# Order of the ffn's first products by parts of x, and epsilon as a bias of the layernorm's root

## Chip, core, metric

One core of one Trainium2 chip runs the whole program. The engines are TensorE (PE in the profile; PEld are its weight loads), VectorE (DVE), ScalarE (ACT), GpSimd (POOL) and SyncE (SP, which only issues transfers here). The metric is device time in microseconds for one execution; several executions are made, and the median counts. The outputs must agree with the reference.

## What is computed

x has 2048 rows of 256 numbers, float32. It is normalized row by row, and attention (16 heads of 128) and a small gated ffn with three-valued weights both read the normalized x; both are added to x.

```python
def _layernorm(x, axis=-1, eps=1e-05):
    m = jnp.mean(x, axis=axis, keepdims=True)
    v = jnp.var(x, axis=axis, keepdims=True)
    return (x - m) / jnp.sqrt(v + eps)
...
def _quantize(w):
    gamma = jnp.mean(jnp.abs(w))
    return jnp.clip(jnp.round(w / (gamma + EPS)), -1.0, 1.0)

def _bitlinear(x, w):
    return jnp.matmul(x, _quantize(w).T)
x1 = _bitlinear(x, w1)
x2 = _bitlinear(x, w2)
hidden = jax.nn.sigmoid(x1) * x2
return _bitlinear(hidden, w3)
...
xn = _layernorm(x, axis=-1)
x = x + _L0_attn_ref(xn, L0_attn_Wqkv, L0_attn_Wout) + _L0_ffn_ref(xn, L0_ffn_w1, L0_ffn_w2, L0_ffn_w3)
```

w1 and w2 are 704 x 256, w3 is 256 x 704.

## The kernel before

Rows of x go in four blocks (c = 0 to 3) of 512 (QB), each of four tiles (t) of 128 rows. Everything runs inside a manual schedule: each engine executes its instructions in the order in which the Python code writes them, and waits where it needs another engine's result.

**The start.** `loads` issues the transfers of x and the weights. GpSimd fills a few constants, among them `ident`, the identity matrix for transposes (filled by a memset and a select, masks.py lines 197 and 199) and `ones`. TensorE runs 20 transposes of `ident` into a tile `idle` (L539), whose result nobody reads. `normalized` (L381 and on) makes xn of a block or of half a block: the statistics of each row tile (`bn_stats` L388, `bn_aggr` L389) give mean and variance in `mv`; `ve` is variance plus epsilon (L392, VectorE); `sd` is its root (L394, ScalarE); `r0` is the reciprocal (L396), and one Newton step (L398 to L401), which reads ve again, gives `rstd`; L405 writes xn. It is called five times: for tiles 0 and 1 of block 0, for its tiles 2 and 3, and once for each of the blocks 1, 2 and 3. `turned` transposes xn on TensorE (pxn, L416), and ScalarE copies the result into xnT (L420). Pieces of the first heads' v, q and k are written between these calls (L229, L116, L106), with copies on ScalarE (L235, L121, L110). Meanwhile VectorE quantizes w1, w2 and w3 to w0q, w1q and w2q (`quantize`, L446 to L462), the means of their absolute values coming from ScalarE (L431) and a small product (pg, L438).

**The ffn.** Products of the ffn are made with two parts of each float32 operand: the cast to a shorter type (the high part, xh, L477, ScalarE) and what is left (the low part, xl, L478, VectorE). `halved_x(0)` makes them for block 0, before w3 is quantized and after k piece 0. The ffn has 24 chunks (c, f): four blocks by six slices f of the hidden dimension, 128 wide, where the last slice holds the 64 left of both weights. For each, `hidden` makes ph: for the two weights (j = 0, 1, into the two banks of one PSUM tile) four products each, over the two halves d of the 256 inputs and the two parts i of x (i = 0 high, i = 1 low). In before the order is j outermost, then i = 1 before i = 0, then d, so that the low parts come first (L495). A sigmoid on ScalarE (L501) and a product on VectorE (L502) follow, and the result is halved again (hidh, hidl). `summed` multiplies it with w2q into two banks, pf e = 0 and e = 1 (L518), and runs two chunks behind `hidden`: after the chunks 0 and 1 come k pieces 2 and 3, after chunk 2 comes `summed` of chunk 0. The two banks of pf are those that k pieces 2 and 3 used before; ScalarE's copies of these (kT, L110) set them free. The sg and hid tiles lie in a pool that is opened when the pool of the raw weights is closed, so their first writer waits until the quantization has read the raw weights.

**The attention** follows with 64 blocks of queries (16 heads by 4 blocks): scores (L612), maximum (L617), exponential (L627), an exchange of quarter tiles through DMA (L646), transposition (L680), the product with v (L690), and next heads' products between them. ScalarE's table of functions is loaded three times in all: for the first root, the first sigmoid, and for the exponential before the attention.

The sqrt in L394 takes ve with the default bias, a constant in the instruction.

Of the kernel before, what the change touches and what calls it, by code (L numbers as in the profile page):

```python
# [8 lines left out]
F32 = mybir.dt.float32  # L9
F32R = mybir.dt.float32r  # L10
AF = mybir.ActivationFunctionType
# [3 lines left out]
LN_EPS = 1e-05  # L15
# [4 lines left out]
def layernorm_attention_bitffn_kernel(  # L20
# [14 lines left out]
    nc = tc.nc  # L35
    P = 128
# [5 lines left out]
    KC = DM // P  # L42
# [89 lines left out]
    ws, ts = {}, {}  # L132
# [195 lines left out]
    fw = front.enter_context(tc.tile_pool(name="ffw", bufs=1))  # L328
# [13 lines left out]
    def loads(fraw):  # L342


        def load_x(c: int, lo: int, hi: int, queue):
            queue.dma_start(
                ys[c][:, lo:hi],
                x[c * QB + lo * P : c * QB + hi * P, :].rearrange("(t p) d -> p t d", p=P),
            )

        load_x(0, 0, 1, nc.sync)
        load_x(0, 1, 2, nc.scalar)
        load_weights(0, "v")
        load_x(0, 2, TB, nc.scalar)
        load_x(1, 0, 2, nc.sync)
        load_x(1, 2, TB, nc.scalar)
        load_weights(0, "q")
        load_x(2, 0, TB, nc.sync)
        load_x(3, 0, TB, nc.sync)
        raw = []  # L360
        for i, src in enumerate((w1T, w2T)):
            w = fraw.tile([P, KC, FF], F32, tag=f"w{i}", name=f"w{i}s")
            nc.sync.dma_start(w, src.rearrange("(c p) f -> p c f", p=P))
            raw.append(w)
        w = fraw.tile([P, FC, DM], F32, tag="w2", name="w2s")
        whole = FF // P
        rest = FF - whole * P
        if rest:
            nc.gpsimd.memset(w[:LAST, whole, :], 0.0)
        nc.sync.dma_start(  # L370
            w[:, :whole, :], w3T[: whole * P, :].rearrange("(c p) e -> p c e", p=P)
        )
        if rest:
            nc.sync.dma_start(w[LAST:, whole, :], w3T[whole * P :, :])
        raw.append(w)
        load_weights(0, "k")
        return raw

    xns = {}

    def normalized(fraw, c: int, t0: int = 0, t1: int = TB):  # L381

        y = ys[c]
        m = t1 - t0
        mv = fraw.tile([P, m, 2], F32, tag=f"mv{m}", name=f"mv{c}_{t0}", bufs=2)
        for t in range(t0, t1):
            st = fraw.tile([P, 6], F32, tag="st", name=f"st{c}_{t}", bufs=4)
            nc.vector.bn_stats(st, y[:, t, :])  # L388
            nc.vector.bn_aggr(mv[:, t - t0, :], st)  # L389

        ve = fraw.tile([P, m], F32, tag=f"ve{m}", name=f"ve{c}_{t0}", bufs=2)
        nc.vector.tensor_scalar(ve, mv[:, :, 1], LN_EPS, None, ALU.add)  # L392
        sd = fraw.tile([P, m], F32, tag=f"sd{m}", name=f"sd{c}_{t0}", bufs=2)
        nc.scalar.activation(sd, ve, AF.Sqrt)  # L394
        r0 = fraw.tile([P, m], F32, tag=f"r0{m}", name=f"r0{c}_{t0}", bufs=2)
        nc.vector.reciprocal(r0, sd)  # L396
        e0 = fraw.tile([P, m], F32, tag=f"e0{m}", name=f"e0{c}_{t0}", bufs=2)
        nc.vector.scalar_tensor_tensor(e0, ve, -0.5, r0, ALU.mult, ALU.mult)  # L398
        nc.vector.tensor_tensor(e0, e0, r0, ALU.mult)
        rstd = fraw.tile([P, m], F32, tag=f"rstd{m}", name=f"rstd{c}_{t0}", bufs=2)  # L400
        nc.vector.scalar_tensor_tensor(rstd, e0, 1.5, r0, ALU.add, ALU.mult)  # L401
        if t0 == 0:
            xns[c] = fraw.tile([P, TB, DM], F32, tag="xn", name=f"xn{c}")
        for t in range(t0, t1):
            nc.vector.tensor_scalar(  # L405
                xns[c][:, t, :], y[:, t, :], mv[:, t - t0, 0:1], rstd[:, t - t0 : t - t0 + 1],
                ALU.subtract, ALU.mult,
            )

    def turned(c: int, t0: int = 0, t1: int = TB):  # L410


        pt = ps_s.tile([P, KC, QB], F32, tag="s", name=f"pxn{c}_{t0}")
        for d in range(KC):
            for t in range(t0, t1):
                nc.tensor.transpose(  # L416
                    pt[:, d, bass.ts(t - t0, P)], xns[c][:, t, bass.ts(d, P)], ident
                )
        m = (t1 - t0) * P
        nc.scalar.copy(xnT[:, :, c * QB + t0 * P : c * QB + t0 * P + m], pt[:, :, :m])  # L420
# [5 lines left out]
    def magnitude(fraw, i: int, w):  # L426

        wf = w.rearrange("p c f -> p (c f)")
        scratch = fraw.tile([P, FC * DM], mybir.dt.bfloat16, tag="abs", name=f"abs{i}")
        asum = fraw.tile([P, 1], F32, tag=f"asum{i}", name=f"asum{i}")  # L430
        nc.scalar.activation(scratch[:, : wf.shape[1]], wf, AF.Abs, accum_out=asum)  # L431
        asums.append(asum)
# [40 lines left out]
    xs, hids, yTs = {}, {}, {}  # L473
    assert 2 * (FF % P) == P

    def halved(high, low, full):
        nc.scalar.copy(high, full)  # L477
        nc.vector.tensor_tensor(low, full, high, ALU.subtract)  # L478
# [7 lines left out]
    def hidden(fp, c: int, f: int):  # L486
        ph = ps_s.tile([P, 2, QB], F32, tag="s", name=f"ph{c}_{f}")
        todo = [(d, i) for i in (1, 0) for d in range(KC)]
        if f == FC - 1:
            ws = [quantized["last"]]  # L490
        else:
            ws = [quantized[j][:, :, bass.ts(f, P)] for j in range(2)]
        for j, w in enumerate(ws):
            for d, i in todo:
                nc.tensor.matmul(  # L495
                    ph[:, j, :], w[:, d], xs[c][i][:, d],
                    start=((d, i) == todo[0]), stop=((d, i) == todo[-1]),
                )
        p0 = LAST if f == FC - 1 else 0
        sg = fp.tile([P, QB], F32, tag="sg", name=f"sg{c}_{f}", bufs=2)  # L500
        nc.scalar.activation(sg[p0:], ph[: P - p0, 0, :], AF.Sigmoid)  # L501
        nc.vector.tensor_tensor(sg[p0:], sg[p0:], ph[p0:, len(ws) - 1, :], ALU.mult)  # L502
        hid = [fp.tile([P, QB], F32R, tag=f"hid{i}", name=f"hid{i}{c}_{f}", bufs=4) for i in "hl"]
        halved(hid[0][p0:], hid[1][p0:], sg[p0:])
        hids[c, f] = hid
# [24 lines left out]


    with tc.manual_schedule():
        nc.gpsimd.memset(ones, 1.0)
        for i in range(2):
            nc.gpsimd.memset(rinvs[i][0], 0.0)

        idle = ps_s.tile([P, 2, QB], F32, tag="s", name="idle")
        for i in range(20):
            nc.tensor.transpose(idle[:, i % 2, :P], ident, ident)  # L539
        with tc.tile_pool(name="fraw", bufs=1) as fraw:  # L540
            raw = loads(fraw)

            normalized(fraw, 0, 0, 2)
            turned(0, 0, 2)
            normalized(fraw, 0, 2, TB)
            v_piece(0, 0)
            turned(0, 2, TB)
            normalized(fraw, 1)
            q_piece(0, 0)
            v_piece(0, 1)  # L550
            turned(1, 0, 2)
            turned(1, 2, TB)
            q_piece(1, 0)
            normalized(fraw, 2)
            magnitude(fraw, 0, raw[0])
            v_piece(0, 2)
            q_piece(0, 1)
            magnitude_of_all(0)
            turned(2, 0, 2)
            turned(2, 2, TB)  # L560
            v_piece(0, 3)
            normalized(fraw, 3)
            quantize(fraw, 0, raw[0])
            magnitude(fraw, 1, raw[1])
            v_piece(0, 4)
            q_piece(0, 2)
            magnitude_of_all(1)
            turned(3)
            quantize(fraw, 1, raw[1])
            magnitude(fraw, 2, raw[2])  # L570
            v_piece(0, 5)
            k_piece(0, 0)
            magnitude_of_all(2)
            halved_x(0)
            quantize(fraw, len(raw) - 1, raw[-1])
        k_piece(0, 1)
        fp = front.enter_context(tc.tile_pool(name="ffn", bufs=2))
        chunks = [(c, f) for c in range(NB) for f in range(FC)]
        for i, (c, f) in enumerate(chunks):
            hidden(fp, c, f)  # L580
            if f == 2 and c + 1 < NB:
                halved_x(c + 1)
            if i < 2:
                k_piece(0, i + 2)
            else:
                summed(fp, *chunks[i - 2])

        warm = small.tile([P, 1], F32, tag="warm", name="warm", bufs=1)
        nc.scalar.activation(warm, ident[:, 0:1], AF.Exp)
# [342 lines left out]
    with tc.manual_schedule():  # L932
        for u in range(-LEAD, (NBK - 1) * TB):
# [12 lines left out]
            g, i = divmod(n, GB)  # L946
            if n >= NB and t < 2:
                i, j = divmod(i, NB)
                j = 2 * j + t
# [127 lines left out]
```

## Time and profile before

| what | us |
|---|---|
| median of 3 runs (lowest, highest) | 2242.94 (2241.7, 2243.55) |
| the profiled execution's own time | 2243.99 |
| its span, first to last instruction | 2242.2 |
| from the start to the ffn's first product | 34.69 |
| ffn: start of its first product to start of its last | 34.69 to 104.80 |
| table load of L394, of L501 (each) | 1.28 |
| mean of the five roots (L394) | 0.206 |

A row of the timeline has the start and the duration of an instruction (or of several alike), its engine, its line, its operation, the tiles written and read, and in brackets how long the engine was idle before it and what released it; "issue" means that it waited for nothing that the profile shows. Starts are microseconds from the start of the span. Matmuls overlap: the duration of one is longer than the distance to the next, so rates are read from the starts.

### The profile page before, as it was taken

What the parts mean: (1) busy time and instruction counts of PE and PEld (TensorE: products, weight loads), DVE (VectorE), ACT (ScalarE), POOL (GpSimd) and SP (SyncE); (2) the same over time, 40 slices, a digit from 0 to 9 for tenths busy, and PEclk for the clock granted to TensorE, in tenths of its full rate; (3) what the DMA queues carried; (4) which work ended last, traced back from release to release, by engine and by line L of the source; (5) the groups of instructions that cost most, each with busy time, mean ns of one, the idle gap of its engine ahead of it and who ended that gap; (6) DMA issues with size and microseconds to landing.
All of it is one profiled execution on the core that took longest, in us unless ns stands there. A gap on an engine that the chain in (4) does not pass through costs nothing.

```text
span 2242.2 us, 24572 instructions
## 1 busy us (share of the span) xinstructions
PE 2230.5 (99%) x5434; PEld 1025.3 (46%) x5434; DVE 1772.0 (79%) x2329; ACT 652.4 (29%) x1138; POOL 681.1 (30%) x1223
## 2 busy tenths in 40 slices
PE   9999999999999999999999999999999999999999
PEld 6744444444444444444444444444444444444445
DVE  6577778888788878888788878788778887888876
ACT  5543222222222222222222222222222222222231
POOL 0021144231452223522234313332134221452442
PEclk9999999999999999999999999999999999999999
DMA  2166666775676666676666766667566676676775
GB/s 91 50 161 172 156 166 172 186 195 157 165 196 179 185 159 164 188 203 169 155 176 179 197 179 150 176 181 199 163 166 179 175 197 159 158 200 181 197 202 145
DMA packets 252515, 382.72 MB, mean 171 GB/s; under 512 B 86224, under 2 KB 90768, under 8 KB 252368
## 3 DMA queue, kind: packets, MB, share of 16 engines
q1 hardware_dynamic: 127664, 174.95, 30.3%
q10 hardware_dynamic: 74896, 101.94, 17.2%
q0 software_dynamic: 49808, 104.27, 16.6%
q8 instruction: 43, 0.70, 0.1%
q14 instruction: 104, 0.85, 0.1%
HBM read 62.98 MB, written 34.73 MB: 44 GB/s over the span
## 4 chain that ended last, share of the span: by engine, by line
PE 67%; DMA 16%; DVE 7%; SPq 5%; issue 2%; ACTq 2%; ACT 1%; DVEq 0%; POOL 0%
PE s L612 26%; PE av L690 25%; DMA part<-p 16%; PE pw L166 5%; SPq L646 5%; DVE pT L680 3%; PE pvw L280 3%; PE pow L783 3%; PE ph L495 2%; ACTq L646 2%; DVE mx L617 1%; PE pf L518 1%; ACT p L627 1%; DVE osums L790 1%; PE pv L229 1%
## 5 line engine op out<-in xcount | busy, mean ns | idle before, releaser
L627 ACT ACTIVATE p<-s,nm 128x1024 f32<-128x1024 f32 x512 | 566.1, 1110 | 1512.5 <-DMA part<-p 1269.5
L612 PE MATMUL s<-kT,qT 128*128 128x512 f32 x2048 | 922.5, 593 | 2.6 <-ACT p L627 2.4
L617 DVE TENSOR_REDUCE mx<-s 128x1 f32<-128x1024 f32 x512 | 623.6, 1221 | 353.5 <-PE s L612 353.3
L690 PE MATMUL av<-pT,v 128*128 128x512 f32 (+1 forms) x1952 | 888.4, 585 | 0.0
L680 DVE STREAM_TRANSPOSE pT<-part 128x1024 f32<-128x1024 f32 x512 | 605.2, 1220 | 37.3 <-DMA part<-p 31.1
L612 PEld LDWEIGHTS s<-kT,qT 128*128 128x128 f32 x2048 | 388.3, 190 | 493.6 <-issue 474.7
L690 PEld LDWEIGHTS av<-pT,v 128*128 128x128 f32 x1952 | 370.9, 190 | 450.2 <-issue 448.0
L665 POOL DMA_DIRECT2D rd<-r x240 | 124.9, 527 | 616.8 <-DVE r L663 614.0
L311 POOL DMA_DIRECT2D xnT<-v x448 | 221.1, 501 | 84.9 <-DVE v L304 54.4
L723 POOL TENSOR_TENSOR o<-o 128x512 f32<-128x512 f32 x56 | 71.2, 1271 | 198.6 <-PE pow L783 168.4
L708 POOL DMA_DIRECT2D od<-oT x60 | 34.1, 568 | 300.5 <-DVE oT L701 300.5
L790 DVE TENSOR_TENSOR osums<-pow,osums 128x512 f32<-128x512 f32 x196 | 124.2, 675 | 0.0
L627 ACT ACTIVATION_READ_ACCUMULATOR p<-s,nm 128x1 f32 x512 | 100.3, 196 | 0.0
L166 PE MATMUL pw<-t,ws 128*128 128x512 f32 x168 | 86.6, 597 | 1.0 <-DVE kT L193 1.0
L189 DVE TENSOR_TENSOR kT<-pw,kT 128x512 f32<-128x512 f32 x112 | 74.7, 667 | 0.0
L304 DVE TENSOR_TENSOR v<-pvw,v 128x512 f32<-128x512 f32 x98 | 65.5, 680 | 0.1
L690 PE MATMUL av<-pT,osums 128*128 128x512 f32 x128 | 59.5, 592 | 0.0
L186 DVE SCALAR_TENSOR_TENSOR qT<-pw,qT 128x512 f32<-128x512 f32 x84 | 57.5, 684 | 0.1
L166 PE MATMUL pw<-xnT,wk 128*128 128x512 f32 x112 | 57.2, 592 | 0.0
L783 PE MATMUL pow<-o,wos 128*128 128x512 f32 x112 | 57.2, 592 | 0.0
L166 PEld LDWEIGHTS pw<-t,ws 128*128 128x128 f32 x168 | 31.0, 189 | 44.1 <-issue 34.0
L620 DVE TENSOR_REDUCE nm<-mx 128x1 f32<-128x2 f32 x256 | 39.7, 155 | 13.4
(140 smaller groups left out, 1146.6 us busy)
## 6 DMA issues: line engine op xcount, KB each, us to landing
part<-p SPq DMA_DIRECT2D x2556, 64.0 KB, 2.2
part<-p ACTq DMA_DIRECT2D x1540, 64.0 KB, 2.5
oT<-rd POOLq DMA_DIRECT2D x60, 256.0 KB, 4.1
od<-oT POOLq DMA_DIRECT2D x60, 256.0 KB, 3.3
o<-od POOLq DMA_DIRECT2D x60, 256.0 KB, 4.5
xnT<-v POOLq DMA_DIRECT2D x448, 32.0 KB, 2.4
osums<-yd POOLq DMA_DIRECT2D x28, 512.0 KB, 5.4
yd<-osums POOLq DMA_DIRECT2D x28, 512.0 KB, 4.7
```

The costliest lines, as they stand in the source:

```text
L166: nc.tensor.matmul(pm, lhs, rhs, start=True, stop=True)
L189: nc.vector.tensor_tensor(k, pk, base, ALU.add)
L311: nc.gpsimd.dma_start(v_part[q // 2][bass.ts(j, 32), bass.ts(q % 2, S // 8)], v[bass.ts(q, 32), bass.ts(j, S // 8)],)
L612: nc.tensor.matmul(s[:, bass.ts(j, QB)], qTs[h, b][:, bass.ts(t, P)], kTs[h][:, i * HALF + j * QB : i * HALF + (j + 1) * QB], start=True, ...
L617: nc.vector.tensor_reduce(mx[:, i : i + 1], s, AX.X, ALU.max)
L627: nc.scalar.activation(p, s, AF.Exp, bias=nm, accum_out=sums[n][:, t, i : i + 1],)
L646: queue.dma_start(parts[v][g // 2][bass.ts(j, 32), g % 2, :], ps[j // 2][bass.ts(g, 32), bass.ts(j % 2, S // NQ)],)
L665: nc.gpsimd.dma_start(rds[n % 2][:, bass.ts(j, 32)], riT[32 * j : 32 * j + TB, :])
L680: nc.vector.transpose(pTs[n][:, t, 2 * i : 2 * i + 2], part)
L690: nc.tensor.matmul(av, v_tile(h)[:, v_place(h, k), :], pTs[n][:, t0:t1].rearrange("p t g (k q) -> p (t g) k q", q=32)[:, :, k, :], start=( ...
L783: nc.tensor.matmul(pm, lhs, o3[:, i], start=True, stop=True)
L790: nc.vector.tensor_tensor(y, pm, y, ALU.add)
```

## The change

In `normalized` the root reads the variance in mv itself, and epsilon is added by ScalarE as the instruction's bias, from a tile eps of one number in each partition. GpSimd writes eps with a memset, the first instruction of the manual schedule. ve is still computed. In `hidden` the first chunk alone, (0, 0), takes its products in another order: all four products with the high part xh (both weights, both d), then all four with the low part xl. The two weights' sums thus alternate between their banks. All other chunks keep their order.

```diff
     xns = {}
+    eps = fw.tile([P, 1], F32, tag="eps", name="eps")
...
         nc.vector.tensor_scalar(ve, mv[:, :, 1], LN_EPS, None, ALU.add)
         sd = fraw.tile([P, m], F32, tag=f"sd{m}", name=f"sd{c}_{t0}", bufs=2)
-        nc.scalar.activation(sd, ve, AF.Sqrt)
+        nc.scalar.activation(sd, mv[:, :, 1], AF.Sqrt, bias=eps)
...
         todo = [(d, i) for i in (1, 0) for d in range(KC)]
+        if (c, f) == (0, 0):
+
+            todo = todo[KC:] + todo[:KC]
         if f == FC - 1:
             ws = [quantized["last"]]
         else:
             ws = [quantized[j][:, :, bass.ts(f, P)] for j in range(2)]
-        for j, w in enumerate(ws):
-            for d, i in todo:
-                nc.tensor.matmul(
-                    ph[:, j, :], w[:, d], xs[c][i][:, d],
-                    start=((d, i) == todo[0]), stop=((d, i) == todo[-1]),
-                )
+        order = [(j, *di) for j in range(len(ws)) for di in todo]
+        if (c, f) == (0, 0):
+            order.sort(key=lambda a: a[2])
+        for j, d, i in order:
+            nc.tensor.matmul(
+                ph[:, j, :], ws[j][:, d], xs[c][i][:, d],
+                start=((d, i) == todo[0]), stop=((d, i) == todo[-1]),
+            )
...
     with tc.manual_schedule():
+        nc.gpsimd.memset(eps, LN_EPS)
         nc.gpsimd.memset(ones, 1.0)
```

## The prediction

> **What bounds the kernel now.** I read the page first: span, busy times, chain, groups.
>
> ```profile
> span 2242.2 us, 24572 instructions
> PE 2230.5 (99%) x5434; PEld 1025.3 (46%) x5434; DVE 1772.0 (79%) x2329; ACT 652.4 (29%) x1138; POOL 681.1 (30%) x1223
> ```
>
> PE is busy 99% of the span. Busy times by stage say where it is not: from 0 to 34.69 us PE works 30.67 us; from there to 104.80 (the rest of the ffn) 70.11 of 70.11; after that 2129.69 of 2137.40. So a microsecond that PE gains or loses before 34.69 reaches the end, unless a wait behind it swallows it. The change touches only the first 45 us, which I read next, in the timeline (columns: start, duration, engine, line, operation, tiles, in brackets the idle time before and its releaser).
>
> ```profile
> 2.22 1.28 ACT L394 ACT_TABLE_LOAD   x1 [2.22 <-issue]
> ...
> 4.23 0.18 DVE L389 BATCH_NORM_AGGREGATE mv<-st 128x2 f32<-128x6 f32 x1
> 4.44 0.17 DVE L392 TENSOR_SCALAR ve<-mv 128x2 f32<-128x2 f32 x1
> 4.65 0.20 ACT L394 ACTIVATE sd<-ve 128x2 f32<-128x2 f32 x1 [1.14 <-DVE ve L392]
> 4.88 0.17 DVE L396 RECIPROCAL r<-sd 128x2 f32<-128x2 f32 x1 [0.27 <-ACT sd L394]
> ...
> 6.14 1.23 PE L416 MATMUL pxn<-ident,xn 128*128 128x128 f32 x4
> ```
>
> The first layernorm is a chain of tiny steps, and the chain of waits runs through all of them: mv, ve, root, reciprocal, xn, the transposes at 6.14, the copy of xnT at 7.40, the v products at 8.04; from 11.26 on that chain is nothing but PE until 31.82. The root's table load (1.28 us) waits for nothing: it runs at 2.22, while x is still on its way, and is over 1.1 us before the root can start.
>
> ```profile
> 32.33 1.05 ACT L477 CAST xh<-xnT 128x1024 fp32r<-128x1024 f32 x1
> ...
> 33.41 1.23 DVE L478 TENSOR_TENSOR xl<-xnT,xh 128x1024 fp32r<-128x1024 f32 x1 [0.36 <-ACT xh L477]
> ...
> 34.69 0.73 PE L495 MATMUL ph<-xl,w0q 128*128 128x512 f32 x2 [0.94 <-DVE xl L478]
> ...
> 36.04 1.82 DVE L462 SCALAR_TENSOR_TENSOR w2q<-w2s,pos,low 128x1536 fp32r<-128x1536 f32 x1
> ...
> 37.96 1.28 ACT L501 ACT_TABLE_LOAD   x1 [3.59 <-DVE w2q L462]
> ...
> 39.25 0.60 ACT L501 ACTIVATE sg<-ph 128x512 f32<-128x512 f32 x1
> ...
> 43.49 0.58 ACT L110 COPY kT<-pk 128x512 f32<-128x512 f32 x1
> ...
> 44.12 0.19 PEld L518 LDWEIGHTS pf<-hidl,w2q 128*128 128x128 f32 x1 [0.16 <-ACT kT L110]
> ```
>
> PE waits 0.94 us for xl although xh is there 1.3 us earlier. And a second gate stands 9.4 us behind: the third matmul of pf0 needs the bank that kT's last copy frees at 44.07. Note also the sigmoid's table load: there it **does** wait for a DVE result, w2q, ending at 37.86.
>
> **Part 1, the high parts first.** Eight matmuls stay eight, with the same tiles; no instruction is added but a wait or two that were met long before (w1q ended at 32.79). The last k product starts at 33.16 and takes 0.43 (four in 1.72), so the first high product can start at 33.6, xh having landed at 33.38. Four at 0.23 (starts 35.49, 35.72, 35.95) end at 34.51; the low ones wait for xl until 34.69 as now, start at 34.69, 35.03, 35.26, 35.49, and the next k product starts at 35.72 instead of 36.65: PE gains 0.93 there. What is late next is the gate at 44.12. Its copy on ACT is the end of a chain that PE does not set: w2q to 37.86, table load 37.96, sigmoid 39.25, product on DVE 39.88, hidh 40.61, kT 41.13, sigmoid 41.61, hidh 42.96, kT 43.49. No member of it moves with the order of PE. Now PE comes to this weight load 0.11 late at most (its matmul starts at 44.23, as 0.23 after 44.00 it would anyway); afterwards PE comes 0.93 early, waits, and restarts at 44.12 with a bare weight load (0.34 to the next start, as at 34.69 to 35.03), so the fourth starts at 44.46, as today. Worth: 0.93 if that gate were not there, 0.00 to 0.11 with it; I take **0.0**.
>
> **Part 2, epsilon as the bias.** It removes one link: the root reads mv (there at 4.41), not ve (4.61). ve stays, since L398 needs it, but runs beside the root. That is 0.20 us earlier. A bias read from a tile has its price: Exp with a bias tile takes 1.11 us for 1024 columns (L627), the cast and the copy without one 1.05 and 1.01, so 0.06 to 0.10, taken as 0.08, on a root of 0.20.
>
> It also adds a wait. The root now waits for DVE (mv) and, the first time, for POOL (the memset of eps). The data are no matter (POOL is done by 1.1 us); the place of the wait is. In the program of before an instruction carries one wait itself and the others stand as separate semaphore instructions ahead of it; wherever DVE and POOL are both awaited (over a hundred instructions, on PE above all) it is DVE's that is split off and POOL's that stays. And a table load stands directly before its activation, behind the split-off waits: that is the 37.96 row, released by w2q and not by issue. So the first root becomes: wait for mv, load the table, root. From 4.41: 0.10 to the load (37.86 to 37.96), 1.29 to the activation (37.96 to 39.25), 0.28 for it, 0.03 to the reciprocal (4.85 to 4.88): 6.11 instead of 4.88, **1.23 us later**. Bounds: 0.02 for the first hop, 1.28 and 0.26 give 1.11; 0.30 for the root gives 1.25. Queued behind it on ACT are xnT's copy and the later roots, which need this root anyway; DVE stands at the reciprocal with y's next statistics behind it, PE at the transposes. All shift alike, so xh, xl, w2q and both gates of part 1 shift too. The other four roots need no POOL wait: the one at 12.02 waits for ve and would gain 0.1, but its transposes wait for PE (xn ends at 14.52, they start at 14.81); the others wait behind ACT copies.
>
> [...]
>
> **The clock of PE.** The 20 warm-up transposes end at 6.01 and the real ones start at 6.14. Four take 1.23 there, four take 0.60 at 9.87: PE turns to full speed in between. With the delay PE idles from 6.01 to 7.37 just there. The v products (x8, 1.73) could then run at half speed, 1.73 more; or the turn shifts along and costs nothing. PE also idled 0.67 before 8.04 and kept or got its speed, so nearer to nothing: I take 0.2, bounds 0 and 1.7. [...]
>
> **At nothing:** the memset of eps, 0.1 to 0.2 us on POOL (rows of 0.10 and 0.20) ahead of ident's fill, moves the warm-up's end to at most 6.21, hidden while the transposes wait until 7.37; without the delay it would cost up to 0.2. eps takes a few bytes of a pool that is closed before the attention, whose tiles stay where they are.
>
> **Sum:** span 2242.2 + 1.23 + 0.2 - 0.0 = 2243.6. That execution took 2243.99 in all, 1.05 above the median of 2242.94; on the median the forecast is 2242.94 + 1.43 = **2244.4**.
>
> **Rivals.**
> 1. The load stays early (the split-off wait is POOL's). For it: the present row at 2.22, with one wait only. Against: the pairs of DVE and POOL, and the 37.96 row. Then the root gains 0.20 - 0.08 = 0.12, but the transposes can start at 6.02 only if the warm-up is over, now 6.01 plus up to 0.2. Net -0.1 to +0.1: 2242.9. Chance 0.12.
> 2. The gate at 44.12 gives way, for example because kT's copy comes earlier than I read, and the 0.93 of part 1 is kept: 2244.4 - 0.9 = 2243.5. Against it stand all nine links above. Chance 0.06.
> 3. The other side, slower: the idle gap in the warm-up keeps PE at half speed far longer. To pass 0.2% (4.5 us) over 1.23, PE must lose 3.3 more, that is run at half speed for 6.6 us more, from the first v product (8.04 + 1.23 = 9.27) to about 15.9. From there on it decides; with 7.5 us of it the time is 2242.9 + 1.2 + 3.8 = 2248. For it: part of the first 5 us of PE is half speed; against it: PE is nearly full again from 7.37 on. Chance 0.05.
>
> **How the numbers follow.** Forecast 0.75, rivals 0.12, 0.06 and 0.05; 0.02 for something that no row shows, of either sign. 0.2% of 2243 is 4.5 us, about what a measurement of this kernel can tell from no change; forecast and rivals 1 and 2 lie inside it. Same 0.93, slower 0.055, faster 0.015. The range: below, rival 1 less half of the runs' spread (2241.7 to 2243.55), 2242.1; above, the forecast with the whole half-speed stretch, 2242.94 + 1.25 + 1.7 and the spread, 2247.0.
>
> **What would show it.** After: the first table load of L394 released by DVE, at about 4.5, root at 5.8, reciprocal at 6.1, transposes at 7.4; ph's first matmul at about 34.8 (33.6 shifted) reading xh; a weight load of pf waiting about 0.9 for kT (L110) near 45.4; the last stage unchanged in length. The prediction is wrong if the load stays at 2.2, if pf's wait is missing, or if the attention stage alone differs by more than 2 us.

## The result and the profile after

The changed kernel takes 2246.88 us (median of 18 runs, 2244.5 to 2249.29) against 2243.11 us for the kernel before measured beside it (18 runs, 2241.28 to 2247.53). The ratio is 1.0015 with a 95% interval of 1.0009 to 1.0021, so the change costs 3.8 us by the medians and 3.4 by the ratio, at least 2.0 and at most 4.7. The forecast was 2244.4, within 2242.1 to 2247.0. The mechanism that it named is there; one of its terms, the clock's, was much too small.

The page first. It looks like before, but the span is 2.8 us longer:

```profile
span 2245.0 us, 24574 instructions
PE 2232.3 (99%) x5434; PEld 1026.1 (46%) x5434; DVE 1772.5 (79%) x2329; ACT 652.9 (29%) x1138; POOL 679.1 (30%) x1224
```

The timeline of the first 14 us shows where (line numbers are those of the changed file: the root is L395, the reciprocal L397, the real transposes L417):

```profile
4.31 0.18 DVE L390 BATCH_NORM_AGGREGATE mv<-st 128x2 f32<-128x6 f32 x1
4.52 0.17 DVE L393 TENSOR_SCALAR ve<-mv 128x2 f32<-128x2 f32 x1
4.57 1.28 ACT L395 ACT_TABLE_LOAD   x1 [4.57 <-DVE mv L390]
5.87 0.30 ACT L395 ACTIVATE sd<-mv,eps 128x2 f32<-128x2 f32 x1
6.20 0.17 DVE L397 RECIPROCAL r<-sd 128x2 f32<-128x2 f32 x1 [1.50 <-ACT sd L395]
...
7.45 0.87 PE L417 MATMUL pxn<-ident,xn 128*128 128x128 f32 x4 [1.41 <-DVE xn L406]
...
9.00 3.10 PE L229 MATMUL pv<-wv,xnT 128*128 128x256 f32 x8 [0.68 <-ACT xnT L421]
...
11.89 1.06 PE L417 MATMUL pxn<-ident,xn 128*128 128x128 f32 x4
...
13.63 1.98 PE L116 MATMUL pq<-xnT,wq 128*128 128x512 f32 x4 [0.68 <-ACT xnT L421]
```

The table load has gone from 2.22 to 4.57, and its bracket now names mv: it stands behind the data. The reciprocal starts 1.32 us later than before, 0.08 of which is x, which landed later in this execution. Then follow the same rows: the transposes start 1.31 late, the v products only 0.96 (this time the transposes already ran at the full clock, 0.87 instead of 1.23), but the q product after them 2.37. Between 9.00 and 13.63 something new has happened. The busy times by stretch tell what it is (columns: stretch, its length, busy time of PE, PEld, DVE, ACT and POOL, granted TensorE clock, DMA share, GB/s):

```profile
6.32:9.72 3.40, 1.59 (x7) 1.12 (x8) 2.92 (x14) 0.78 (x2) 0.00 (x0) 1.00 1.07 356
9.73:13.13 3.40, 3.23 (x10) 2.24 (x8) 3.07 (x12) 0.78 (x3) 0.00 (x0) 0.50 1.05 395
13.14:20.00 6.86, 6.37 (x26) 4.18 (x27) 4.21 (x17) 2.89 (x8) 0.00 (x0) 1.00 0.54 161
```

TensorE had full speed, lost it for one stretch of 3.4 us, and had it again afterwards. The eight v products took 3.10 us (before 1.99) because most of them fell into that stretch: from 9.32 on they start 0.22 us apart, from 9.76 on 0.43.

In these two executions nothing is won back later. The first score product of the attention starts at 101.99 (before 99.56), 2.43 later; the last product of the attention with v is 2.83 later. Part 1 can be read at its gate:

```profile
35.89 0.78 PE L501 MATMUL ph<-xh,w0q 128*128 128x512 f32 x2
...
36.28 0.42 PEld L501 LDWEIGHTS ph<-xh,w1q 128*128 128x128 f32 x2
36.50 0.63 PE L501 MATMUL ph<-xh,w1q 128*128 128x512 f32 x2
...
37.15 0.30 PEld L501 LDWEIGHTS ph<-xl,w0q 128*128 128x128 f32 x2 [0.46 <-DVE xl L479]
...
45.95 0.58 ACT L110 COPY kT<-pk 128x512 f32<-128x512 f32 x1
...
46.58 0.50 PE L524 MATMUL pf<-hidl,w2q 128*128 128x512 f32 x1 [0.65 <-ACT kT L110]
```

TensorE no longer waits for xl with all eight products in front of it: four run without waiting, and the wait shrinks from 0.94 us to what lies between the fours. But at 46.58 it waits 0.65 us for kT's last copy, where it had no idle time before. From xh's start to the first score product it is 101.99 - 34.79 = 67.20 us; before, 99.56 - 32.33 = 67.23. Of 0.93 us gained, 0.03 is left.

### The profile page after: what moved, and what is told of

It is laid out like the page before. It is cut to its first block, busy times and chain, and to the rows that moved or that the text cites. A ratio compares the mean times of both kernels' runs of the same rounds, so it can differ in the third digit from the quotient of the medians.

```text
span 2245.0 us, 24574 instructions
## 1 busy us (share of the span) xinstructions
PE 2232.3 (99%) x5434; PEld 1026.1 (46%) x5434; DVE 1772.5 (79%) x2329; ACT 652.9 (29%) x1138; POOL 679.1 (30%) x1224
## 4 chain that ended last, share of the span: by engine, by line
PE 80%; DMA 8%; DVE 5%; SPq 3%; issue 1%; ACT 1%; POOL 1%; ACTq 0%; DVEq 0%
PE av L697 32%; PE s L619 31%; DMA part<-p 8%; PE pw L166 7%; PE pvw L280 4%; SPq L653 3%; PE pow L790 3%; DVE pT L687 2%; PE ph L501 2%; DVE mx L624 1%; PE pf L524 1%; DVE osums L797 1%; PE pv L229 1%; PE pq L116 0%; DVE v L319 0%
```

## The experiments

Each edit is against the kernel before or against the changed kernel, as said. Totals are compared with runs of the kernel before on the same chip at the same time: 2242.73 for the first four experiments, 2243.37 for the last four (33 runs each). Because totals scatter by a few us, the place of events within the profiled execution is read beside them. Differences in us are those of the medians; the ratio and its interval can differ from them by some tenths of a us, up to 1 us.

### Part 1 alone

The changed kernel without eps:

```diff
-    eps = fw.tile([P, 1], F32, tag="eps", name="eps")
...
-        nc.scalar.activation(sd, mv[:, :, 1], AF.Sqrt, bias=eps)
+        nc.scalar.activation(sd, ve, AF.Sqrt)
...
-        nc.gpsimd.memset(eps, LN_EPS)
```

> Part 1 alone (high parts first, root as before). Theory (part 1 is swallowed at the bank that kT's last copy frees, part 2's late table load costs everything): root at 4.65, PE 0.9 ahead at k piece 2, then a wait of about 0.6 to 0.9 for kT before the third matmul of pf0; the attention's first score product at 99.56 plus or minus 0.1; total within 1 us of before. Rival (the new order itself costs: the two banks in alternation slow the eight products or what follows): first score product more than 1 us later and the total 2 to 4 us up.

Measured: 2243.36 us, ratio 1.0002 (0.9993 to 1.0011). From xh to the first score product 99.23 - 32.03 = 67.20. TensorE's waits in the first 100 us (columns: what waits, for whom, us, times, longest):

```profile
...
PE pq L116 <- ACT xnT L420: 0.8, 1, 0.8
PE pv L229 <- ACT xnT L420: 0.7, 1, 0.7
PE pf L523 <- ACT kT L110: 0.7, 1, 0.7
...
```

The wait for xl has gone from the list and one for kT has come. Within the interval part 1 neither costs nor brings anything. (The first score product itself is at 99.23, 0.33 before the kernel before and outside the expected 99.56 plus or minus 0.1: in this execution the full clock came earlier, at 5.81 instead of 7.36, and the first real transposes took 0.87 instead of 1.23.)

### Part 2 alone

The kernel before with eps, filled by GpSimd, as the root's bias:

```diff
+    eps = fw.tile([P, 1], F32, tag="eps", name="eps")
...
-        nc.scalar.activation(sd, ve, AF.Sqrt)
+        nc.scalar.activation(sd, mv[:, :, 1], AF.Sqrt, bias=eps)
...
+        nc.gpsimd.memset(eps, LN_EPS)
```

> Part 2 alone (epsilon as the root's bias, filled by GpSimd; products in the old order). Theory: all of the change's loss: table load behind mv at 4.5, reciprocal 1.2 to 1.3 later, ratio to before as the whole change's (about 1.0015, 1.2 to 1.3 us from the load and the rest from a colder TensorE clock). Rival (part 1 costs): less than half of the change's loss, 1.2 us or less in total.

Measured: 2246.00 us, ratio 1.0012 (1.0003 to 1.0021), 3.3 us over before. Table load at 4.53, reciprocal at 6.15, and again one stretch at half clock, here from 8.99 to 12.41:

```profile
4.53 1.28 ACT L395 ACT_TABLE_LOAD   x1 [4.53 <-DVE mv L390]
...
6.15 0.17 DVE L397 RECIPROCAL r<-sd 128x2 f32<-128x2 f32 x1 [1.50 <-ACT sd L395]
...
8.95 3.68 PE L229 MATMUL pv<-wv,xnT 128*128 128x256 f32 x8 [0.67 <-ACT xnT L421]
```

```profile
9.00:12.40 3.40, 3.40 (x8) 2.69 (x9) 3.03 (x13) 0.09 (x1) 0.00 (x0) 0.50 1.07 394
```

The first score product is at 102.21, as late as in the changed kernel. With part 1 alone at no difference, the loss is part 2's, as far as the intervals can tell.

The profiled execution also shows what a single total is worth. It took 2243.97 us, the lowest of its eleven and as much as that of the kernel before (2243.99), though its first score product came 2.65 later: its attention stage, from the first score product to the last product with v, took 2134.82 us, that of the kernel before 2137.50 and that of the changed kernel 2137.90. Nothing in that stage was edited. It differs by up to 3.1 us between the ten profiles, without regard to the edits.

### Who fills eps

The changed kernel, one word different:

```diff
-        nc.gpsimd.memset(eps, LN_EPS)
+        nc.vector.memset(eps, LN_EPS)
```

> The whole change, but eps filled by VectorE, so that the first root waits for VectorE alone. Theory (the load stands behind the wait that is split off because two engines are awaited): load back at about 2.2 with no wait, reciprocal at about 4.8 (0.12 before 4.88), total at before or up to 0.3 us under it. Rival (a bias read from a tile is what sends the load behind the data): load at about 4.5 again, total as the whole change's.

Measured: 2242.27 us, ratio 0.9997 (0.9989 to 1.0006). Its timeline:

```profile
0.82 0.06 DVE L539 MEMSET eps<- 128x1 f32 x1 [0.82 <-PEq L1065]
...
2.22 1.28 ACT L395 ACT_TABLE_LOAD   x1 [2.22 <-issue]
...
4.42 0.30 ACT L395 ACTIVATE sd<-mv,eps 128x2 f32<-128x2 f32 x1 [0.92 <-DVE mv L390]
4.74 0.17 DVE L397 RECIPROCAL r<-sd 128x2 f32<-128x2 f32 x1 [0.16 <-ACT sd L395]
```

The load is back at 2.22, released by nothing, with the same bias from a tile. So it is not the bias that sends the load behind the data, but the second engine to be waited for: with mv and eps both from VectorE the load waits for nothing, and the root alone waits, 0.92 us for mv. The reciprocal starts at 4.74, 0.14 before 4.88 (x landed 0.03 earlier here), as the part's idea promises. The transposes start at 6.00 instead of 6.14, but at the attention's first score product (99.53) only 0.03 of this is left, and the total, 0.5 us under before, cannot be told from no change.

The views of the profile leave out semaphore instructions; the trace has them. In the changed kernel one of L395 stands on ScalarE at 4.52, for 0.02 us, ahead of the load at 4.57: it waits for VectorE's semaphore, and the root itself waits for GpSimd's. In this run's rows nothing stands ahead of the load, and the root, at 4.42, is released by VectorE's mv.

### The warm-up made longer

The changed kernel, with the idle transposes reaching up to the real ones:

```diff
-        for i in range(20):
+        for i in range(27):
```

> The whole change with 27 instead of 20 idle transposes, which end at about 7.3 and fill TensorE's gap before the first real ones. Theory (the part of the loss beyond 1.24 is the clock, lost because TensorE idles from 6.05 to 7.45 while it is being judged): no stretch at half clock after the first 8 us, mean clock 1.000 in the records, total 1.0 to 1.6 us over before. Rival (the half-clock stretch has nothing to do with that gap): mean clock 0.997 to 0.999 as in the change, total 3 to 4 us over before.

Measured: 2243.10 us, ratio 1.0003 (0.9994 to 1.0012). The root is as late as in the changed kernel (reciprocal at 5.99, with x 0.21 earlier), yet only 0.4 us of the loss is left; the profiled execution has no half-clock stretch after the first grant of full clock, and all eleven executions show a mean clock of 1.000. The real transposes and the v products:

```profile
7.25 0.87 PE L417 MATMUL pxn<-ident,xn 128*128 128x128 f32 x4 [0.82 <-DVE xn L406]
8.80 1.99 PE L229 MATMUL pv<-wv,xnT 128*128 128x256 f32 x8 [0.68 <-ACT xnT L421]
```

1.99 us is what the v products took before; in the changed kernel it was 3.10. TensorE still idles 0.82 us here, because at full clock, which came at 5.15, the added transposes were over sooner than planned. The first score product is at 100.40, 0.84 after that of before. The total came out below the expected 1.0 to 1.6 us over before, though its interval (-1.3 to +2.7 us) holds that too.

### The gap alone

The kernel before, root unchanged, with a shorter warm-up, so that TensorE idles before the real transposes and nothing else is late:

```diff
-        for i in range(20):
+        for i in range(14):
```

> The kernel before with 14 instead of 20 idle transposes, so that TensorE idles from about 4.7 to 6.14 with nothing else late. Theory (an idle gap of some 1.4 us in the first 7 us costs the clock): a stretch of 3.4 us at half clock among the first 14 us, or full clock granted one stretch later, mean clock 0.997 to 0.999, total 1.5 to 3 us over before. Rival (a gap alone is harmless, the late root is what counts): clock 1.000 and total within 0.5 us of before.

Measured: 2245.99 us, ratio 1.0016 (1.0007 to 1.0025), 2.6 us over before. The reciprocal is on time (4.99), but:

```profile
6.25 1.23 PE L416 MATMUL pxn<-ident,xn 128*128 128x128 f32 x4 [1.52 <-DVE xn L405]
8.15 3.78 PE L229 MATMUL pv<-wv,xnT 128*128 128x256 f32 x8 [0.67 <-ACT xnT L420]
11.72 0.98 PE L416 MATMUL pxn<-ident,xn 128*128 128x128 f32 x4
```

Full clock comes at 12.48 in this execution, and the q product starts at 13.37 instead of 11.26. An idle gap of 1.5 us costs as much as a good part of the whole change without making any input late. (The clock of this profile reads 1.000 and not 0.997 to 0.999 as expected: the records begin with the first grant of full clock, and what lies before is not in the mean. The products show it: the eight v products took 3.78 us, before 1.99.)

### The gate opened

Two kernels have one more instruction behind k piece 1, a sigmoid of one column that nobody reads, so that the sigmoid's table comes while ScalarE waits for w2q; first the kernel before with it, then part 1 with it:

```diff
         k_piece(0, 1)
+        early = small.tile([P, 1], F32, tag="warm", name="early", bufs=1)
+        nc.scalar.activation(early, ident[:, 0:1], AF.Sigmoid)
```

> The kernel before with one added sigmoid of a single column behind kT's copy of k piece 1, so that the sigmoid's table is loaded at about 34.4 while ScalarE waits anyway. The gate at pf0 opens 1.3 earlier, but TensorE, in the old order, does not come earlier. Theory: xh's start to the attention's first score product 67.1 to 67.25 (before 67.23), total as before. Rival (the chain through the sigmoids bounds more of the ffn than this gate): more than 0.4 us shorter.

> Part 1 (high parts first, root as before) together with the early sigmoid table. Theory (part 1's 0.93 is swallowed at the bank that kT's last copy frees, a copy that the sigmoid's late table holds up): no wait for kT at pf0, xh's start to the attention's first score product 66.3 (0.9 shorter than 67.2), total about 0.9 us under order_only, which the runs can barely tell. Rival (the 0.93 is swallowed elsewhere, or the next gate stands right behind): 67.0 to 67.25.

Measured: the early table alone 2243.02 us, ratio 1.0001 (0.9992 to 1.0010), from xh to the first score product 99.28 - 32.09 = 67.19. With part 1: 2242.07 us, ratio 0.9994 (0.9986 to 1.0003), 98.80 - 32.53 = 66.27. ScalarE and the weight loads of pf in the latter:

```profile
34.60 1.28 ACT L583 ACT_TABLE_LOAD   x1
35.89 0.20 ACT L583 ACTIVATE early<-ident 128x1 f32<-128x1 f32 x1
38.18 0.60 ACT L506 ACTIVATE sg<-ph 128x512 f32<-128x512 f32 x1 [2.08 <-DVE w2q L462]
...
42.42 0.58 ACT L110 COPY kT<-pk 128x512 f32<-128x512 f32 x1
```

```profile
43.06 0.19 PEld L523 LDWEIGHTS pf<-hidh,w2q 128*128 128x128 f32 x1
43.28 0.19 PEld L523 LDWEIGHTS pf<-hidl,w2q 128*128 128x128 f32 x1
43.51 0.19 PEld L523 LDWEIGHTS pf<-hidh,w2q 128*128 128x128 f32 x1
```

kT's copy is over at 43.00, and the third weight load, at 43.28, waits for nothing. Part 1 alone brings 0.03, the early table alone 0.04, both together 0.96: neither is worth anything without the other. In the totals 0.9 us is below what these runs can tell from nothing.

### Both repaired

The changed kernel with eps filled by VectorE and the early sigmoid table.

> The whole change with eps filled by VectorE and the early sigmoid table. Theory: reciprocal at about 4.75, xh's start to the first score product 66.3, total 0.5 to 1.5 us under before. Rival (nothing is left of either gain): total as before, within 0.3 us.

Measured: 2242.70 us, ratio 0.9999 (0.9990 to 1.0007); reciprocal at 5.01 (the root's input came 0.27 later than in the run under "Who fills eps"), xh to the first score product 98.45 - 32.19 = 66.26. It is better than the changed kernel by some 4 us. Against the kernel before, the gain is seen in the trace (the first score product at 98.45 instead of 99.56, part of which is the clock's earlier turn: the first real transposes took 0.87 us here, 1.23 before) and not in the total.

## What the clock follows

The records of the granted clock begin with the first grant of full clock. What lies before it is called half by the pace of the products: in the kernel before, where that grant stands at 7.36, four real transposes took 1.23 us from 6.14 on and 0.60 at 9.87. Two profiles show more than one change of the clock in the first 15 us. In the changed kernel it is full from 6.31, half from 9.72 and full again from 13.14; in part 2 alone the three changes stand at 5.58, 8.99 and 12.41. The changes thus lie 3.41 us apart in both. The table has the busy time of TensorE in the 3.41 us ahead of the first grant and in the 3.41 us behind it:

| profile | first grant | PE busy of the 3.41 ahead | PE busy of the 3.41 behind | clock after these |
|---|---|---|---|---|
| before | 7.36 | 3.28 | 2.44 | full |
| part 1 alone | 5.81 | 3.41 | 2.52 | full |
| part 1, early table | 7.49 | 3.07 | 2.51 | full |
| changed | 6.31 | 3.14 | 1.59 | half |
| part 2 alone | 5.58 | 3.41 | 1.20 | half |
| longer warm-up | 5.15 | 3.41 | 2.15 | full |
| shorter warm-up | 12.48 | 3.41 | - | full |

The clock went back to half in the two profiles with 1.59 and 1.20 us, and stayed full in the four with 2.15 to 2.52. In the half-clock stretches of the first two, TensorE was busy for 3.23 and 3.40 us, and full clock followed. The shorter warm-up, in which TensorE idled 1.52 us before the real transposes, has the latest first grant. That the clock goes by TensorE's busy time over such a stretch is the author's reading of these few rows; no run shows how it is decided.

So the changed kernel makes TensorE idle 1.41 us, then work 0.87, then idle 0.68, in the 3.7 us up to the change of the clock at 9.72, and runs the next 3.41 us at half clock. Its 18 executions show mean clocks from 0.997 to 1.000; the eight at 0.998 or less have a median of 2247.4 us, the other ten 2246.5. The mean sorts them only in part, since it misses whatever half clock lies ahead of the first grant.

## Why the prediction was right, and where it was off

**The late table load**: right, and for the reason given. Forecast 1.23 us, load at about 4.5, root at 5.8, reciprocal at 6.1, transposes at 7.4; measured 1.24 (1.32 less 0.08 of x), at 4.57, 5.87, 6.20 and 7.45. The root took 0.30, the upper of the two ends. From the load's start to the root's it took 1.30 us, so no more than the load itself stood in between. Rival 1, the load staying early, is what happens when VectorE fills eps. The premise on the waits holds in the trace of the kernel before: apart from the semaphore instructions none carries more than one wait, and wherever VectorE and GpSimd are both awaited it is VectorE's that is split off. By its records these places number 58, however, 54 of them on TensorE, and not over a hundred.

**Part 1 at 0.0**: right. 0.03 was left, and TensorE waited where the forecast put it (near 45.4, shifted by the clock to 46.58); forecast 0.9, measured 0.65 on the products and 1.07 on the weight loads. The early table shows that the gate was the only thing that swallowed it: 0.96 with the gate open. Rival 2 falls. ph's first product came at 35.89 and not at 34.8, since all that lies ahead of it, xh included, came 2.46 later and not 1.23.

**The clock**: this is the term that failed, "nearer to nothing: I take 0.2, bounds 0 and 1.7". From the start of the v products to the start of the q product it is 3.22 us in all seven profiles in which full clock, once granted ahead of the v products, stays; it is 4.63 in the changed kernel, 4.90 in part 2 alone and 5.22 in the shorter warm-up, so 1.4, 1.7 and 2.0 more. In the totals the gap alone brought 2.6 us, and part 2 alone and the longer warm-up, both with the late root, differ by 2246.0 - 2243.1 = 2.9 us. Two things were wrong. The bound counted the v products alone, though the transposes behind them run at half speed too (0.98 instead of 0.60 in the shorter warm-up). And the choice between the bounds went by one row, an idle time of 0.67 us that did no harm: in the profiles here it is the busy time of TensorE over the 3.41 us behind the grant that sorts the cases, 1.59 and 1.20 us against 2.15 and more. Rival 3 named the right cause, the idle gap, though it asked for 6.6 us more at half speed where the profile shows 3.41; the result, 2246.88, is nearer to its 2248 than to the forecast's 2244.4.

**The sum**: 1.43 was forecast and 3.77 measured. The forecast's other terms hold in the traces; of what is missing, the start shows the clock's part. From the first statistics of x to the first score product the changed kernel takes 101.99 - 3.32 = 98.67 us, part 1 alone 99.23 - 3.29 = 95.94: 2.73 more, of which the late root is 1.24 and the stretch at half clock 1.41. The profiled execution of the kernel before is 0.38 slower here than part 1 alone (99.56 - 3.24 = 96.32), because full clock came only at 7.36 and its first real transposes ran at half speed; against it the difference is 2.35. The late root is paid in full: the longer warm-up, which has it without the loss of clock, takes 100.40 - 3.11 = 97.29, 1.35 more than part 1 alone. That 2246.88 lies inside the range, 0.1 under its upper end, is partly luck: the terms themselves end at 2242.94 + 1.25 + 1.7 = 2245.9, and only the runs' spread on top of them reaches further.

**The root without ve** for the later calls, and **the memset of eps**: at nothing, as forecast (the warm-up began 0.03 us later, 1.51 instead of 1.48).

**The sign in the attention stage**, a difference of more than 2 us, was too narrow: the stage differs by up to 3.1 us between profiles in which nothing of it was changed. Here it differed by 0.40.

Open: where the rest of the 3.8 us lies. The two profiled executions differ by 2.9 us because that of the kernel before took 0.9 more than the median of its runs (2243.99 and 2243.11), while that of the changed kernel stands at its median (2246.85). Its start explains 2.4 to 2.7 us, which the interval of 2.0 to 4.7 holds. The mean clocks, down to 0.997, say that some executions spend more than 3.41 us at half clock (3.41 of 2245 us is a mean of 0.999); no such execution was traced.

## What to carry to other kernels

Where an activation has a table load ahead of it, look at what it waits for. With one engine to wait for, the load stood in idle time here, at 2.22; with two it stood behind the data, at 4.57, and that was 1.24 us on the path. The engine that filled a constant thus decided over the critical path, though the constant was ready at 0.99. A wait taken away on TensorE is worth what the next gate leaves of it (0.03 of 0.93 us here, 0.96 with the gate open), so follow the chain to that gate before moving products. And a gap in the first microseconds can cost more in clock than in waiting: one of 1.5 us, with no input late, cost 2.6 us of the total here.

## What was not expected

How close the two outcomes of the clock lie in the few profiles here: behind the first grant, 3.41 us with TensorE busy for 1.59 us were followed by half clock, 3.41 us with 2.15 us were not. And that six idle transposes fewer in an otherwise unchanged kernel (1.48 to 4.73 instead of to 6.01) cost 2.6 us of 2243 (ratio 1.0007 to 1.0025).
